# A four-layer image network on one core: layer norm of an MLP in a written order, and image norms moved from the spectra to the window attention

## The chip, the core and the metric

The kernel runs on one NeuronCore of a Trainium2 chip. The time is the device time of one execution in microseconds, the median of a few runs. The engines are PE (TensorE matmul, with PEld for its weight loads), DVE (VectorE), ACT (ScalarE), POOL (GpSimd) and SP (SyncE), which issues most of the DMAs. [...]

## The reference

Four images of 56 x 56 pixels with 128 channels go through four residual layers, `x = x + layer(group_norm(x))`, in float32.

```python
x = x + L0(_gn(x), ...)   # 7x7 window attention, then LayerNorm + global attention over 3136 tokens,
                          # then LayerNorm, 128->512, exact gelu, 512->128 (the MLP)
x = x + L1(_gn(x), ...)   # edge layer: relu(p_i + p_j + be) summed over j in each row of 56, node = relu(...)
x = x + L2(_gn(x), ...)   # Fourier neural operator with attention over the 56 rows as time steps
x = x + L3(_gn(x), ...)   # 3x1 convolution, row and column sums, relu
```

`_gn` is a group norm over 32 groups of 4 channels. In L2 each row of the image is one 56 x 128 field; it is instance-normed once more (`_inorm`), transformed with `rfft2` of 56 x 128, weighted, and compared with the other rows in an attention. So what L2 needs first of every image is its group norm, the mean and deviation of each row, and the spectra of its rows.

## The kernel before, in words

The image lies with its 128 channels on partitions and its 3136 pixels behind one another. `build` (L2368) first loads the inputs and takes their group norms, and then branches once: where the attention scores are small (they are with these inputs) it runs `first_layers` (L2416) for each of the four samples. What is inside the branch is scheduled by itself, and what follows it starts behind it. Per sample:

- **Windows**, `fast_windows` (L305): the image in 8 groups of 392 pixels (8 windows of 7x7). Ten small stages (`norm`, `project`, `score`, `value`, `turn`, `output`, `central`, `variance`, `attended`, `divide`) are issued in a skewed order, turn n working on groups n+2 down to n-11 (L467 to L471). PE, ACT and DVE keep that order as it is written (`manual_schedule`); POOL and SP are ordered by the framework's scheduler. The stages share three PSUM banks (`bank`, L348). Twice, at groups 3 and 7, `variance` takes the roots of four groups together (L434), one Sqrt on ACT and one reciprocal on DVE.
- **Global attention**, the rest of `fast_attention` (L560).
- **MLP**, `mlp` (L848), in 8 parts of 392 pixels. First the layer norm of all parts: `centre` (L676: a product with the centring matrix and a Square on ACT), a copy to `y` on ACT (L874), `inverse_deviation` (L684: a product that sums the squares, a Sqrt, a reciprocal on DVE, L692) and a multiply on DVE (L877). Then per part: `hidden` (L860, four products and four gelu), four products into `po` (L885), the bias and both residuals (L886) and three adds that put the windows back into image rows (L892 to L895), and statistics of the part (L896) for the next group norm. Only PE's order is written by hand; ACT and DVE are ordered by the scheduler.
- **Edge layer**, `edge_layer` (L905). Its result `x1` is stored to DRAM as `x2d[b]` by an SP DMA (L2424).

After the four samples come L2 and L3. SP loads weights; POOL makes the score weights (`all_score_weights`, L1393) and the value weights (`value_weights`, L1337), which end in a store `dd` on SP's queue (L1365). `spectra` (L1309) takes sample 3 first, whose `x1` is still in SBUF, then 0, 1 and 2, which are loaded from `x2d` (L1203). For each sample `normed_images` (L1188) does:

- statistics of each of the 56 rows (L1209), aggregated (L1213) to the group norm's mean and root (two products with `k.g4`, L1215 and L1231, Sqrt at L1233),
- the group norm in place in one instruction (L192, called at L1236) and a store to `xad[b]` (L1237),
- from the same row statistics the second norm of each row, `st.norm` (products at L1243 and L1249, Sqrt at L1251).

`sample_spectra` (L1258) then makes the **first transform** (L1267 to L1276: 224 small products of one row each, scaled by `st.norm` into `z`), and after it products into `S` and `iS` (L1281), `R` (L1293) and `xh` (L1303), evacuated by ACT and DVE. While one sample's spectra are issued, the next sample's norm is advanced by one step per chunk (L1332). PE, ACT and DVE keep the written order. Behind it come the attention weights (`attention_weights`, L1405, products L1471), `attend` (products L1594) and `outputs` (L2311).

## Time and profile before

The median of three runs is 3901.99 us (3901.64 to 3906.46). The profiled execution took 3907.5 us, with a span of 3905.7 us from the first to the last instruction, 79417 instructions and a mean granted PE clock of 0.954.

| stage | from - to, us | PE busy | DVE busy | ACT busy | POOL busy |
|---|---|---|---|---|---|
| inputs, norms, branch | 0 - 53 | 23.9 | 30.5 | 15.2 | 0.2 |
| windows, sample 0 | 53 - 155 | 91.0 | 54.1 | 47.6 | 8.7 |
| global attention, sample 0 | 155 - 542 | 365.2 | 325.9 | 290.9 | 0 |
| MLP, sample 0 | 542 - 607 | 59.1 | 39.3 | 33.5 | 0 |
| edge layer, sample 0 | 607 - 760 | 146.1 | 129.5 | 83.1 | 112.9 |
| windows, sample 3 | 2174 - 2271 | 87.6 | 48.7 | 48.3 | 3.7 |
| MLP, sample 3 | 2654 - 2716 | 56.2 | 39.4 | 33.0 | 0 |
| norm of sample 3 for L2 | 2870 - 2891 | 2.7 | 16.6 | 0.5 | 8.4 |
| spectra of the four samples | 2891 - 3016 | 93.3 | 68.2 | 34.7 | 29.6 |
| attention weights | 3016 - 3164 | 128.7 | 105.2 | 11.9 | 101.4 |
| attend | 3164 - 3515 | 324.5 | 252.1 | 59.9 | 308.3 |
| outputs | 3515 - 3906 | 347.5 | 225.0 | 144.2 | 221.7 |

A share of busy time tells little of a PE that does many small matmuls, whose ends are modelled; the order in time and the waits tell which engine was late. "L594" is line 594 of the kernel before, "a<-b" means that the instruction writes tile a and reads tile b, and "x56" counts instructions. The clock that was granted to PE is given as a share of full speed.

### The profile page before, as it was taken

How to read it: one execution, taken by the hardware profiler on the slowest of the kernel's cores; microseconds unless marked ns; L12 is line 12 of the kernel's file. 1: busy time of each engine (PE TensorE's matmuls, PEld its weight loads, DVE VectorE, ACT ScalarE, POOL GpSimd, SP SyncE). 2: the span in 40 equal slices, each digit the busy share in tenths (PEclk: the TensorE clock that was granted, in tenths of full speed). 3: DMA queues.
4: the chain of work that ended last, by engine and by line, in shares of the span. 5: the costliest groups of instructions: out<-in, count | busy, mean ns of one | idle time of the engine just before them, and what ended most of it. 6: DMA issues, size and time to landing. Idle time of an engine off the chain costs nothing. (4 is left out here: it accounts for less than half of the span.)

```text
span 3905.7 us, 79417 instructions
## 1 busy us (share of the span) xinstructions
PE 3553.4 (91%) x35416; PEld 1604.1 (41%) x35416; DVE 2891.3 (74%) x2759; ACT 2086.9 (53%) x2108; POOL 1156.6 (30%) x563
## 2 busy tenths in 40 slices
PE   6899989989998899999889999998967989989988
PEld 4432234542323455232245532224446433336564
DVE  6588877758887785888779578886965767775654
ACT  4577765457776544877655467774622012215332
POOL 0000006600000470000027100001851769984656
PEclk8999999999999999999999999999978999999888
DMA  2000000000000000000000000000031048841101
GB/s 95 1 1 1 1 17 2 19 1 1 1 1 1 18 3 18 1 1 1 1 18 3 18 1 1 1 1 1 3 112 61 1 98 177 165 111 70 52 7 50
DMA packets 73497, 111.13 MB, mean 28 GB/s; under 512 B 62140, under 2 KB 63932, under 8 KB 67900
## 3 DMA queue, kind: packets, MB, share of 16 engines
q1 hardware_dynamic: 14460, 93.13, 8.0%
q10 hardware_dynamic: 58688, 12.85, 2.0%
q8 instruction: 280, 4.59, 0.5%
q14 instruction: 69, 0.57, 0.1%
HBM read 79.46 MB, written 26.51 MB: 27 GB/s over the span
## 5 line engine op out<-in xcount | busy, mean ns | idle before, releaser
L651 ACT ACTIVATE f_ring<-f_s 128x1792 f32<-128x1792 f32 (+3 forms) x796 | 1097.7, 1429 | 231.5 <-PE f_s L649 229.6
L594 DVE TENSOR_TENSOR f_acc<-f_acc,f_ring 128x1792 f32<-128x1792 f32 x560 | 1134.0, 2025 | 66.1 <-ACT f_ring L651 9.3
L988 POOL TENSOR_TENSOR e_tp<-e_a,e_c 128x1792 f32<-128x1792 f32 x140 | 451.7, 3259 | 2288.1 <-ACT e_a L951 2183.7
L649 PE MATMUL f_s<-f_qT,f_kT 32*128 32x448 f32 x5376 | 741.4, 574 | 47.8 <-ACT f_ring L651 27.1
L600 PE MATMUL f_po<-f_ring,f_va 128*32 128x448 f32 x5376 | 592.0, 548 | 0.0
L986 DVE TENSOR_TENSOR e_td<-e_pa,e_c 128x1792 f32<-128x1792 f32 x252 | 491.4, 2015 | 14.4 <-ACT e_a L951 14.4
L649 PEld LDWEIGHTS f_s<-f_qT,f_kT 32*128 32x128 f32 x5376 | 269.7, 184 | 526.4 <-ACT f_ring L651 382.5
L993 PE MATMUL e_acc<-e_td,t_shared 32*32 32x448 f32 x8064 | 322.2, 545 | 20.9 <-DVE e_td L986 10.0
L990 ACT ACTIVATE e_tp<-e_tp 128x1792 f32<-128x1792 f32 x140 | 235.1, 1697 | 173.2 <-POOL e_tp L988 173.1
L1589 DVE TENSOR_TENSOR u_ud<-u_px,u_d 112x1792 f32<-112x1792 f32 x144 | 240.1, 1708 | 94.8 <-PE u_po L1594 85.7
L600 PEld LDWEIGHTS f_po<-f_ring,f_va 128*32 128x32 f32 x5376 | 133.5, 109 | 398.0 <-issue 397.0
L993 PE MATMUL e_acc<-e_tp,t_shared 32*32 32x448 f32 x4480 | 220.5, 544 | 3.1 <-ACT e_tp L990 2.5
L1594 PE MATMUL u_po<-u_ud,AT 112*64 112x448 f32 x960 | 200.7, 548 | 23.3 <-DVE u_ud L1589 23.3
L1591 POOL TENSOR_TENSOR u_up<-xh,u_d 112x1792 f32<-112x1792 f32 x64 | 193.8, 3054 | 24.1 <-PE u_po L1594 12.4
L993 PEld LDWEIGHTS e_acc<-e_td,t_shared 32*32 32x32 f32 x8064 | 133.8, 103 | 145.7 <-DVE e_td L986 56.0
L617 DVE RECIPROCAL f_den<-f_den 128x448 f32<-128x448 f32 x28 | 82.7, 2953 | 77.5 <-ACT f_den L616 77.5
L1594 PE MATMUL u_po<-u_up,AT 112*64 112x448 f32 x576 | 125.2, 541 | 0.9 <-POOL u_up L1591 0.9
L1594 PEld LDWEIGHTS u_po<-u_ud,AT 112*64 112x64 f32 x960 | 64.9, 137 | 147.6 <-issue 86.5
L594 DVE TENSOR_TENSOR f_acc<-f_ring 128x1792 f32<-128x1792 f32 x28 | 56.7, 2025 | 90.0 <-ACT f_ring L651 60.3
L865 ACT ACTIVATE m_hT<-m_ph,w_fb 128x392 f32<-128x392 f32 x128 | 72.7, 588 | 83.7 <-PE m_ph L864 78.2
L993 PEld LDWEIGHTS e_acc<-e_tp,t_shared 32*32 32x32 f32 x4480 | 94.4, 103 | 55.3 <-ACT e_tp L990 19.4
L1456 POOL TENSOR_TENSOR q_u<-iS,q_g 128x1792 f32<-128x1792 f32 x32 | 102.8, 3236 | 23.9 <-PE q_acc L1471 23.9
(467 smaller groups left out, 4710.2 us busy)
## 6 DMA issues: line engine op xcount, KB each, us to landing
u_d<-dd SPq DMA_DIRECT2D x48, 784.0 KB
xw<-in_x SPq DMA_DIRECT2D x4, 1568.0 KB
x2d<-x SPq DMA_DIRECT2D x4, 1568.0 KB
x_xs<-xad ACTq DMA_DIRECT2D x32, 196.0 KB
xm<-x_ev ACTq DMA_DIRECT2D x64, 98.0 KB
o_a<-xm SPq DMA_DIRECT2D x8, 784.0 KB
o_x<-x2d SPq DMA_DIRECT2D x4, 1568.0 KB
out<-o_o SPq DMA_DIRECT2D x12, 448.0 KB
```

Of the source, the lines that this page charges most:

```text
L594: nc.vector.tensor_add(acc, slots(j, 0) if c == 1 else acc, slots(j, c))
L600: nc.tensor.matmul(po[heads[h], :NB], va[o, c, heads[h]], p, start=(c == 0), stop=(c == 24))
L649: nc.tensor.matmul(ss[:, i, :NB], kT[heads[h], c * P:(c + 1) * P], qT[heads[h], blk(j)], start=True, stop=True)
L651: nc.scalar.activation(ring[:, slot:slot + m, :], ss[:, :m, :NB], AF.Exp, scale=scale)
L986: nc.vector.tensor_tensor(t, am, cm, ALU.max)
L988: nc.gpsimd.tensor_sub(t, bc(a.rearrange("p (l n) -> p l n", l=8), 1, 4), cm)
L990: nc.scalar.activation(tf, tf, AF.Relu)
L993: nc.tensor.matmul(acc[quarters[q], r, :NB], k.ident[o, o], t[o, q].rearrange("p l n -> p (l n)"), start=(g == 0), stop=(g == len(EDGE_TUR ...
L1456: nc.gpsimd.tensor_mul(u, bc(st.iS[:, bp, c, :HH], 1, HEADS), bc(g[:, n, c, :], 2, HH))
L1589: nc.vector.tensor_mul(u, bc(px[:, :, :NB], 2, m), dm)
L1591: nc.gpsimd.tensor_mul(u, bc(x, 2, m), dm)
L1594: nc.tensor.matmul(po[64 * b2:64 * b2 + 64, :NB], st.AT[:, 8 * i + h0 + q, 2 * bp + b2, :], u[:, b2, q, :], start=(left == 16), stop=(left ...
```

## The change

- **MLP.** PE, ACT and DVE now keep a written order. The layer norm is three functions: `central` (product; parts 0 to 3 are squared by ACT and copied by DVE, parts 4 to 7 copied by ACT and squared by GpSimd from the copy), `deviation` (sum of squares and Sqrt) and `divide` (reciprocal and multiply on DVE). Parts 0 to 2 are divided before the loop over the parts, part wi + 3 in turn wi. A Sqrt of a constant stands ahead of the layer norm and one ahead of the last turn's products. In turns 0 to 6 DVE adds the product, the bias and `xf` in one instruction, and GpSimd adds `xw` and puts the windows into image rows; the statistics of a part come one turn later. The last turn is as before.
- **Image norms.** `normed_images` is split into some fifty steps. For samples 0 to 2 it runs during `fast_windows` of the next sample: one step behind each stage, held back where a step needs a Sqrt until `variance` takes its own. It works in place on `x1` and stores `xad`. `x2d` of samples 0 to 2 is stored behind the edge layer as before; that of sample 3 behind the branch.
- **Spectra.** The order is 0, 1, 2, 3. Normed images of samples 0 to 2 are loaded from `xad` (two at once, the third when a buffer is free); the first two are requested ahead of everything else behind the branch. The norm of sample 3 goes on beside the spectra of samples 0 and 1, three steps per chunk. The first transform is a function of its own, and that of sample b + 1 is issued inside the spectra of sample b, behind chunks 2, 5, 7 and 9. The bank tag `acc` has four buffers for three.

The core of the diff:

```diff
@@ -432,6 +434,7 @@
             if q == HALF - 1:
                 r = wk.tile([P, N], F32, name="w_r")
                 nc.scalar.activation(r, var[:, :N], AF.Sqrt, scale=1024.0, bias=eps)
+                step(True)
                 nc.vector.reciprocal(r, r)
                 roots[g // HALF] = r
...
+        steps = beside(bank)
+        root_next = False
+
+        def step(root):
+            nonlocal root_next
+            if root or not root_next:
+                root_next = next(steps, None) == "root"
+
...
@@ -469,6 +480,7 @@
                              (central, n - 5), (variance, n - 6), (attended, n - 11), (divide, n - 10)):
                 if 0 <= g < NG:
                     stage(g)
+                    step(False)
...
@@ -865,37 +857,88 @@
-        es.enter_context(tc.manual_schedule(engines={mybir.EngineType.PE}))
-        squares = {}
-        for wi in range(9):
+        es.enter_context(tc.manual_schedule(engines={mybir.EngineType.PE, mybir.EngineType.Activation,
+                                                     mybir.EngineType.DVE}))
+        squares, roots = {}, {}
+        root = wk.tile([P, 1], F32, name="m_root")
+        nc.scalar.activation(root, k.eps, AF.Sqrt)
+
+        def central(wi):
+
+            pc = psum.tile([P, 512], F32, tag="mm", name="m_pc", bufs=4)
+            yb = y[:, parts[wi]]
+            nc.tensor.matmul(pc[:, :N], k.centre, xf[:, parts[wi]], start=True, stop=True)
+            squares[wi] = wk.tile([P, N], F32, name="m_sq", bufs=3)
+            if wi < 4:
+                nc.scalar.activation(squares[wi], pc[:, :N], AF.Square)
+                nc.vector.tensor_copy(yb, pc[:, :N])
+            else:
+                nc.scalar.copy(yb, pc[:, :N])
+                nc.gpsimd.tensor_mul(squares[wi], yb, yb)
+
+        def deviation(wi):
+            pv = psum.tile([P, 512], F32, tag="v", name="m_pv")
+            nc.tensor.matmul(pv[:, :N], k.ones_c, squares.pop(wi), start=True, stop=True)
+            roots[wi] = wk.tile([P, N], F32, name="m_r", bufs=8)
+            nc.scalar.activation(roots[wi], pv[:, :N], AF.Sqrt, bias=k.eps)
+
+        def divide(wi):
             if wi < 8:
-                pc = psum.tile([P, 512], F32, tag="mm", name="m_pc", bufs=4)
-                centre(k, wk, pc[:, :N], xf[:, parts[wi]], squares, wi)
-                nc.scalar.copy(y[:, parts[wi]], pc[:, :N])
-            if wi:
-                yb = y[:, parts[wi - 1]]
-                nc.vector.tensor_mul(yb, yb, inverse_deviation(k, wk, psum, squares.pop(wi - 1), 8))
+                r = roots.pop(wi)
+                nc.vector.reciprocal(r, r)
+                nc.vector.tensor_mul(y[:, parts[wi]], y[:, parts[wi]], r)
+        for n in range(10):
+            if n < 8:
+                central(n)
+            if 1 <= n < 5:
+                deviation(n - 1)
+            elif n > 5:
+                deviation(n - 2)
+            if n == 3:
+                divide(0)
+        divide(1)
+        divide(2)
+        def image_rows(wi, i0, i1):
+            r0 = (7 * wi + 3 + i0) % HH
+            return x1[:, r0:r0 + i1 - i0, :]
+
+        def statistics(wi):
+            for i0, i1 in (((0, 7),) if wi < 7 else ((0, 4), (4, 7))):
+                nc.vector.bn_stats(st[:, wi + (i0 > 0), :], image_rows(wi, i0, i1).rearrange("p l n -> p (l n)"))
+
+        def windows(t):
+            return t.rearrange("p (w i j) -> p w i j", w=8, i=7)
         ahead = hidden(parts[0])
         for wi, ts in enumerate(parts):
             hT = ahead
             if wi < 7:
                 ahead = hidden(parts[wi + 1])
+            else:
+
+                nc.scalar.activation(root, k.eps, AF.Sqrt)
             po = psum.tile([P, 512], F32, tag="acc", name="m_po")
             for f in range(4):
                 nc.tensor.matmul(po[:, :N], w.w2[:, f, :], hT[:, f, :], start=(f == 0), stop=(f == 3))
-            nc.vector.scalar_tensor_tensor(xf[:, ts], xf[:, ts], w.b2, xw[:, ts], ALU.add, ALU.add)
-            a = xf[:, ts].rearrange("p (w i j) -> p w i j", w=8, i=7)
-            x = po[:, :N].rearrange("p (w i j) -> p w i j", w=8, i=7)
+            divide(wi + 3)
+            if wi < 7:
+                nc.vector.scalar_tensor_tensor(xf[:, ts], po[:, :N], w.b2, xf[:, ts], ALU.add, ALU.add)
+                if wi:
+                    statistics(wi - 1)
+                add, a, x = nc.gpsimd.tensor_add, windows(xf[:, ts]), windows(xw[:, ts])
+            else:
+
+                nc.vector.scalar_tensor_tensor(xf[:, ts], xf[:, ts], w.b2, xw[:, ts], ALU.add, ALU.add)
+                statistics(6)
+                add, a, x = nc.vector.tensor_add, windows(xf[:, ts]), windows(po[:, :N])
             for i0, i1 in (((0, 7),) if wi < 7 else ((0, 4), (4, 7))):
-                r0 = (7 * wi + 3 + i0) % HH
-                rows = x1[:, r0:r0 + i1 - i0, :]
-                nc.vector.tensor_add(
-                    rows[:, :, 3:52].rearrange("p i (w j) -> p w i j", w=7), a[:, 0:7, i0:i1, :], x[:, 0:7, i0:i1, :])
-                nc.vector.tensor_add(rows[:, :, 52:56], a[:, 7, i0:i1, 0:4], x[:, 7, i0:i1, 0:4])
-                nc.vector.tensor_add(rows[:, :, 0:3], a[:, 7, i0:i1, 4:7], x[:, 7, i0:i1, 4:7])
-                nc.vector.bn_stats(st[:, wi + (i0 > 0), :], rows.rearrange("p l n -> p (l n)"))
-
-        nc.scalar.activation(wk.tile([P, 1], F32, name="m_root"), hT[:, 3, 0:1], AF.Sqrt, bias=k.eps, scale=0.0)
+                rows = image_rows(wi, i0, i1)
+                add(rows[:, :, 3:52].rearrange("p i (w j) -> p w i j", w=7), a[:, 0:7, i0:i1, :], x[:, 0:7, i0:i1, :])
+                add(rows[:, :, 52:56], a[:, 7, i0:i1, 0:4], x[:, 7, i0:i1, 0:4])
+                add(rows[:, :, 0:3], a[:, 7, i0:i1, 4:7], x[:, 7, i0:i1, 4:7])
+        statistics(7)
...
-def normed_images(k, w, st, b, pools, x2d, xad, ready):
+def normed_images(k, w, st, b, wk, bank, xp, xad):
...
+    rows = wk.tile([P, HH, 6], F32, name="s_rows", bufs=1)
     for t in range(HH):
         nc.vector.bn_stats(rows[:, t, :], x[:, t, :])
-        if t % 8 == 7:
+        if t % 2 == 1:
             yield
-    mv = wk.tile([P, 2], F32, name="s_mv")
+    mv = wk.tile([P, 2], F32, name="s_mv", bufs=1)
     nc.vector.bn_aggr(mv, rows.rearrange("p a b -> p (a b)"))
-    ps = psum.tile([P, 512], F32, tag="t", name="s_pt")
+    yield
+    ps = bank()
     nc.tensor.matmul(ps[:, 0:1], k.g4, mv[:, 0:1], start=True, stop=True)
...
     nc.vector.scalar_tensor_tensor(sq, d, HH / 4, sq, ALU.mult, ALU.add)
     nc.vector.tensor_add(mean, half[1], half[4])
+    yield "root"
+    nc.scalar.activation(t1, var, AF.Sqrt, bias=k.eps)
     nc.vector.reciprocal(mr[:, 1:2], t1)
-    apply_norm(k, x, x, mr)
-    nc.sync.dma_start(xad[b], x)
-    ready[b] = xp
-    yield
     nc.vector.tensor_scalar(mean, mean, 0.5, mr[:, 0:1], ALU.mult, ALU.subtract)
     nc.vector.tensor_scalar_mul(mean, mean, mr[:, 1:2])
...
-    nc.scalar.activation(d, ps[:, 128:128 + HH], AF.Sqrt, bias=k.eps)
+    nc.vector.tensor_copy(d, ps[:, 128:128 + HH])
+    yield
+    for t in range(0, HH, 14):
+        apply_norm(k, x[:, t:t + 14, :], x[:, t:t + 14, :], mr)
+        if t == 42:
+            nc.sync.dma_start(xad, x)
+        yield "root" if t == 42 else None
+    nc.scalar.activation(d, d, AF.Sqrt, bias=k.eps)
+    yield
     yield
...
-def sample_spectra(k, st, b, pools, x):
+def first_transform(k, st, b, pools, x, to):
...
-    z = wk.tile([P, 33, 2 * HH], F32, name="s_z")
+    z = to[b] = wk.tile([P, 33, 2 * HH], F32, name="s_z")
...
         yield
+
+
+def sample_spectra(k, st, b, pools, z):
...
-        ps = psum.tile([P, 512], F32, tag="acc", name="s_ps")
+        ps = psum.tile([P, 512], F32, tag="acc", bufs=4, name="s_ps")
...
-def spectra(k, w, st, x2d, xad):
+def spectra(k, w, st, xad, images):
...
-    ready = {}
+    nc.gpsimd.memset(st.x1[:, HH, :], 0.0)
...
-
-        order = [st.last] + [b for b in range(B) if b != st.last]
-        norms = [normed_images(k, w, st, b, (wk, tiny), x2d, xad, ready) for b in order] + [iter(())]
-        next(norms[1])
-        for _ in norms[0]:
+        norm = normed_images(k, w, st, B - 1, wk, lambda: tiny.tile([P, 512], F32, name="s_pt"), st.x1, xad[B - 1])
+        zs = {}
+        first = [first_transform(k, st, b, (wk, psum), st.x1 if b == B - 1 else images(b), zs) for b in range(B)]
+        for _ in first[0]:
             pass
-        for n, b in enumerate(order):
-            ahead = norms[n + 1]
-            for _ in sample_spectra(k, st, b, (wk, psum), ready.pop(b)):
-                next(ahead, None)
-            for _ in ahead:
-                pass
+        for b in range(B):
+            for n, _ in enumerate(sample_spectra(k, st, b, (wk, psum), zs.pop(b))):
+                for _ in range(3):
+                    next(norm, None)
+                if b < B - 1 and n in (2, 5, 7, 9):
+                    next(first[b + 1])
...
@@ -2421,23 +2480,50 @@
                 edge_layer(k, w1, x1, st)
-                nc.sync.dma_start(to, x1)
+                if to is not None:
+                    nc.sync.dma_start(to, x1)
+
+            def norms(b, bank):
+
+                if b < 0:
+                    return iter(())
+                return normed_images(k, w2, st, b, io, bank, x1w, xad[b])
...
             with tc.If(small_scores > 0) as small:
                 for b in range(B):
-                    first_layers(lambda *a: fast_attention(*a, k.mr[:, b, :]), I["x"][b], x2d[b],
-                                 loaded=b == 0)
+                    first_layers(lambda *a: fast_attention(*a, functools.partial(norms, b - 1), k.mr[:, b, :]), I["x"][b],
+                                 x2d[b] if b < B - 1 else None, loaded=b == 0)
...
+        x2s = ExitStack()
+        x2p = x2s.enter_context(tc.tile_pool(name="x2", bufs=2, side="right"))
+
+        def images(b):
+            if b not in loaded:
+                xp = loaded[b] = x2p.tile([P, HH + 1, HH], F32, name="s_x2")
+                for t in range(0, HH, 28):
+                    nc.sync.dma_start(xp[:, t:t + 28, :], xad[b, :, t:t + 28, :])
+                nc.gpsimd.memset(xp[:, HH, :], 0.0)
+            return loaded[b]
+
+        loaded = {}
+        for b in range(2):
+            images(b)
+        nc.sync.dma_start(x2d[B - 1], x1)
         l3p = es.enter_context(tc.tile_pool(name="l3", bufs=1))
         load_weights(k, l3p, I, "w3_", w2)
         load_weights(k, l3p, I, "w2_", w2, only=CONV_WEIGHTS)
-        st = Env()
-        st.x1, st.last = x1w, B - 1
...
                 with tc.tile_pool(name="g_wk", bufs=1, side="right") as wk:
                     all_score_weights(k, I, w2, sp, wk, st)
                     value_weights(k, I, w2, wk, dd)
-                    spectra(k, w2, st, x2d, xad)
+                    spectra(k, w2, st, xad, images)
+                x2s.close()
```

## The prediction

> **What bounds the kernel now.** I read the header of the page first, then busy time by stage, then the order in time inside the three stages that the change touches. The stages by busy time (columns: stretch, its length, then busy us and instructions of PE, PEld, DVE, ACT, POOL, then granted clock, DMA share, GB/s):
>
> ```profile
> 2174.00:2271.00 97.00, 87.59 (x718) 54.32 (x718) 48.73 (x97) 48.34 (x81) 3.65 (x11) 0.96 0.00 1
> 2271.00:2654.00 383.00, 361.04 (x3024) 109.69 (x3024) 325.04 (x168) 290.62 (x221) 0.00 (x0) 1.00 0.00 1
> 2654.00:2716.00 62.00, 56.16 (x164) 31.36 (x164) 39.43 (x66) 33.02 (x61) 0.00 (x0) 0.97 0.00 0
> 2716.00:2870.00 154.00, 146.10 (x3248) 73.31 (x3248) 130.28 (x81) 83.11 (x68) 113.25 (x36) 0.98 0.01 3
> 2870.00:2891.00 21.00, 2.69 (x14) 2.30 (x16) 16.63 (x93) 0.45 (x2) 8.37 (x20) 0.57 0.82 288
> 2891.00:3016.00 125.00, 93.29 (x1224) 83.17 (x1220) 68.21 (x269) 34.68 (x77) 29.64 (x38) 0.75 0.22 85
> ```
>
> These are, for the last sample, windows, global attention, MLP and edge layer, and then, once for all four, the lead-in to the spectra and the spectra. PE is near its limit everywhere but in the last two: there it stands idle for 18 us while DVE norms sample 3, and then works 93 of 125 us at three quarters of its clock. DVE is only half busy in the windows; it is the engine that limits the head of the MLP.
>
> **Part 1, MLP (four times).** In order of time on DVE (start, length, what):
>
> ```profile
> 2660.95 5.06 DVE L692 RECIPROCAL n_r<-n_r 128x392 f32<-128x392 f32 x2
> 2678.55 5.06 DVE L692 RECIPROCAL n_r<-n_r 128x392 f32<-128x392 f32 x2
> 2683.52 0.97 DVE L877 TENSOR_TENSOR m_y<-m_y,n_r 128x392 f32<-128x392 f32 x2
> ```
>
> and on PE, with the idle time before it and its releaser in brackets:
>
> ```profile
> 2667.87 5.64 PE L864 MATMUL m_ph<-m_y,w_f 128*128 128x392 f32 x16
> 2685.24 2.87 PE L885 MATMUL m_po<-m_hT,t_first 128*128 128x392 f32 x8 [1.20 <-DVE x L895]
> ```
>
> Eight reciprocals (2.5 us each) and multiplies (0.5) run without a break from 2660.95 to 2684.4, and only then the first output adds; PE waits for an accumulator bank at 2685.24. From the first hidden product (2667.87) PE needs 8 x 5.27 = 42.2 us (5.27: two groups of eight matmuls, 2675.98 to 2681.25) and takes 44.0, to 2711.8. After the change three divides (9 us) come before the loop and one in each turn. A turn of DVE is 3.0 (divide) + 0.63 (bias and xf, as L886) + 0.56 (L896) = 4.2 us, under PE's 5.27, so the 1.8 us go. At the head ACT loses four of its eight squares, four copies and the Sqrt table load (1.28, now early, in ACT's pause before 2656.3): 0.5 x 8 = 4 us; but PE's own 16 pairs, 2.9 us for the first two and 14 x 0.66, end at 2666.8, and the last sum of squares waits for GpSimd's four squares in a row, until about 2667.4, so only 0.4 us come out. Added: DVE copies (0.57, as L424) of the first four parts, hidden while DVE waits for the first root; GpSimd's squares, 1.0 us each (1.14 for 448 elements at L1351, 1.27 for 512 at L1390), counted just now; GpSimd's adds, 1.4 us a turn, under 5.27. The tail (0.95 us of adds, two statistics) stays. Gain 2.2 us each, **-9** (ends 0 and -14). The next sample's input load now waits for the last add, some 20 us later; it has the edge layer's 154 us to land.
>
> [...] The trace has such a case in the spectra, beside GpSimd's weights, of 56 elements that take 0.21 us elsewhere:
>
> ```profile
> 2909.69 2.95 DVE L1222 SCALAR_TENSOR_TENSOR s_sq<-s_d,s_sq 128x56 f32<-128x56 f32 x1
> 2916.81 2.83 DVE L192 TENSOR_SCALAR s_x<-s_x,s_mr 128x3136 f32<-128x3136 f32 x1
> ```
>
> If each multiply were held by one GpSimd instruction of 1.0 us, [...]a turn of DVE would be 5.2, just PE's pace, and the 1.8 us would still go; held as in the first row (+2.7) a turn is 6.9 and costs 1.6 x 7 = 11 a sample, which makes of -9 some +35. I take neither: GpSimd's add of 1.4 us starts together with the next reciprocal, which reads one tensor and lasts 2.5, so it is over before the multiply. Only the squares can meet a multiply, at the head, where DVE is not late. +35 counts toward the slower cases.
>
> **Part 2, three norms beside the windows (samples 1 to 3).** Each step is emitted behind a stage of the windows, on DVE's, PE's and ACT's fixed orders. DVE: 28 pairs of statistics at 0.32 (0.20 alone, 0.12 more behind another) = 9.0; aggregate 1.67; some 20 small ones at 0.15 to 0.30 = 3.7; reciprocal and scale 0.75; four applies at 0.5 = 2.0: **17.1 us**. PE: four matmuls at 0.4 = 1.6. ACT: two roots at 0.3, placed right behind the windows' own roots, so no table load. The SP queue gets one xad store per sample; behind it stand only the next input load and x2d, which wait for the MLP and the edge layer anyway.
>
> How much is hidden? In groups 3 to 6 of the windows DVE is busy 3.8 of 5.2, 4.0 of 5.6, 4.7 of 6.7 and 4.6 of 7.5 us. The steps that fall there (5, 6, 7 and 7) bring 1.6, 1.9, 2.2 and 3.3: 5.4, 5.9, 6.9 and 7.9, as long as or longer than the group. If DVE can be used to nine tenths, these groups grow by 0.8, 1.0, 0.9 and 1.3 us, the earlier ones by 0.6; PE's waits for the two mean matmuls cost 1.5; the late stretch, where DVE is mostly idle but every multiply (L444) is on PE's path, 2. Together **8 us a sample, +24**. Ends: 3.3 (PE's own 1.6 and as much waiting), and 18.7 when nothing is hidden.
>
> **Part 3, spectra.** Removed: 20.8 us from 2869.9 to the first transform at 2890.7. In its place the stored image is loaded: 1.57 MB at the 300 GB/s of the windows of these microseconds is 5 us, a half of it 2.6; issue at 2871.3 where t_w_qk is issued now, 2 us to land; the first half is there at about 2876. Lead-in 6 us.
>
> The first transform then runs with a cold PE (the granted clock is 0.50 in every stretch from 2874 to 2906). [...] The rows of L1271 (min/median/max ns) speak otherwise:
>
> ```profile
> L1271 PE MATMUL s_pr<-t_images,s_x x672: 222/224/318, 2928.4 to 3001.6; 128*64 128x33 f32 x168
> L1271 PE MATMUL s_pr<-t_images,x x224: 294/295/317, 2890.7 to 2902.6; 128*64 128x33 f32 x112
> ```
>
> The first transform stayed slow from its first to its last product, 12.1 us; later ones, begun warm, take 6.7 to 7.2. I take 12.1[...].
>
> Then the samples. Sample 2, which has no norm beside it, took 18.3 us (2994.6 to 3012.9): 7.2 first transform, 10.3 the rest (0.8 a wait). The next first transform now lies inside the previous sample, so: sample 0 17.0 + 1.7 cold + 4 waiting for sample 3's norm; sample 1 17 + 2; sample 2 17; sample 3 10.3; 3 us for the interleaving. The 4 and 2 come from the waits of PE on a norm's results, some 8.5 us per norm now, against three steps per chunk. Sum: 6 + 12.1 + 22.7 + 19 + 17 + 10.3 + 3 = 90, against 143 (2869.9 to 3012.9). **-53** (ends -60 and -30). GpSimd's weights begin later, since images and x2d go ahead of them on SP's queue (4.7 MB, 16 us), and would end near 2930; the attention weights need them at about 2963.
>
> **Sum.** -9 + 24 - 53 = -38. The profiled execution took 3907.5 (span 3905.7, 1.8 around it): 3869.5. The median of the runs is 5.5 lower, 3902.0: **3864**.
>
> **Rivals.** *Image 2 is stuck behind dd.* SP's queue is in order, and this is how it stood:
>
> ```profile
> 2885.88 0.33 SPq L1237 DMA_DIRECT2D xad<-x  x1
> 2918.02 0.38 SPq L1365 DMA_DIRECT2D dd<-d_f  x1
> 2918.49 1.55 SPq L1288 DMA_DIRECT2D apart<-S  x2
> 2920.09 0.55 SPq L1203 DMA_DIRECT2D s_x<-x2d  x1
> ```
>
> dd waits for GpSimd's last weight, and a load that was free to go stood behind it. If image 2 is queued so again, it is issued at 2918 to 2930, is half there 5 us later, and is wanted at about 2913: 10 to 22 us of waiting, say 15: 3879. Against it: image 2 is requested at the start of the spectra and its buffer is free at 2888. *The windows hide nearly all*: 3.3 for 8, 14 less: 3850. For it: DVE idles half the stage. *They hide nothing*: 18.7 for 8, 32 more: 3896. *Slower*: the steps stretch the windows beyond their DVE time, since a step delays the evacuation that PE waits for, and a norm's product takes one of three banks in rotation. At 0.5 us for each of 50 steps it is 25 a sample, 75 in all: 3902 - 62 + 75 = 3915. It decides from 62/3 = 20.7 us a sample.
>
> **How the numbers follow.** Main case 0.50 (3864); dd 0.27 (3879); all hidden 0.10 (3850); nothing hidden 0.09 (3896); slower 0.04 (3915). A measurement of this kernel can tell about 0.2%, 8 us, from no change. 3896 is at that edge, so half of its chance counts as same, with 0.01 more from the dd case: faster 0.90, same 0.06, slower 0.04. Leaving out the last two cases and going 8 below 3850 and 9 above 3879, for the sizes' own uncertainty: 3842 to 3888.
>
> **What would show it.** Right: windows of samples 1 to 3 some 8 us longer than sample 0's by their own change; MLPs of about 60 us without a wait at the third output product; first transform 6 us behind the edge layer, at half clock; last s_px product near 2963 less the MLPs' and plus the windows' shifts. Wrong: windows of 110 us or more, or a PE wait of over 8 us on a DMA ahead of sample 2's first transform.

## The result, and the profile after

The changed kernel takes **3870.9 us** (3867.4 to 3875.3, 4 runs) against 3901.8 (3899.0 to 3906.5, 4 runs): ratio **0.992, 95% interval 0.990 to 0.994**, so 31 us faster; forecast were 3864 in a range of 3842 to 3888. Its profiled execution took 3875.3 (span 3873.3, before 3905.7): a difference of 32.4.

To see where they are, I cut both spans at PE's own marks: the first attention product `f_s`, the first centring product of the MLP, the first edge product `e_acc` of each sample, and the first product of the attention weights `q_acc`.

| stretch | before | after | difference |
|---|---|---|---|
| start to the first `f_s` | 155.5 | 155.1 | -0.4 |
| `e_acc` to the next sample's `f_s` (edge layer and windows), 3 times | 246.4, 246.0, 248.5 | 258.2, 258.2, 261.6 | **+37.1** |
| `f_s` to the MLP, 4 times | 386.7, 385.7, 386.0, 385.7 | 384.3, 384.4, 384.4, 385.6 | -5.4 |
| MLP to `e_acc`, 4 times | 71.5, 71.3, 71.4, 68.2 | 67.4, 67.4, 67.4, 66.8 | **-13.4** |
| last `e_acc` to `q_acc` (edge layer and spectra) | 293.3 | 236.7 | **-56.6** |
| `q_acc` to the end | 889.5 | 895.8 | +6.3 |

Each column sums to its span. The third and the last stretch have the same code in both kernels. Over all kernels of this study, which leave that code alone, they lie between 384 and 388 and between 884 and 899 us, so -5.4 is scatter of single profiles. The +6.3 need not be scatter alone: with the spectra of before the last stretch takes 889.5 and 883.8 us (before, mlp_only), with the new ones 888.6 to 899.4, ten of eleven above both. DVE, ACT and POOL are as busy there as before, and PE's granted clock in the last 400 us moves between 0.85 and 0.89; what decides it is not shown. The three bold rows are the change.

Busy time by stage for the last sample and the spectra, columns as in the prediction's first fence (stretch, its length, busy us and instructions of PE, PEld, DVE, ACT, POOL, granted clock, DMA share, GB/s):

```profile
2176.50:2288.40 111.90, 94.85 (x732) 57.25 (x732) 68.59 (x183) 48.13 (x82) 8.74 (x22) 0.92 0.07 30
2674.00:2736.50 62.50, 58.03 (x167) 32.66 (x168) 39.36 (x52) 29.84 (x52) 13.21 (x25) 0.94 0.14 52
2888.50:2974.20 85.70, 73.30 (x1208) 64.04 (x1208) 48.65 (x131) 31.40 (x69) 36.10 (x57) 0.88 0.29 100
```

Windows: the norm's own instructions take 15 us of DVE (17.7 if the lengths of their rows are added, as the prediction did), but 43 us of it are still free; PE's granted clock fell from 0.96 to 0.92. Spectra, lead-in included: 85.7 us for what took 143.

**Windows**, PE in order of time, sample 1:

```profile
796.24 0.35 PE L1250 MATMUL w_mm<-s_mv,t_shared 128*128 128x1 f32 x2 [1.51 <-DVE w_rec L399]
...
821.70 0.68 PE L1283 MATMUL w_mm<-s_mean,c_ones_c 128*128 128x56 f32 x2 [4.12 <-DVE s_mean L1279]
822.17 1.64 PE L423 MATMUL w_mm<-xf,c_centre 128*128 128x392 f32 x2
...
844.55 1.49 PE L454 MATMUL w_mm<-w_h,w_fq 128*128 128x392 f32 x2 [1.84 <-DVE w_h L447]
```

PE waits 4.12 us for the row means of a norm, with the windows' own products queued behind. DVE, same stretch, shows what made the means late, a reciprocal of 2.6 us:

```profile
818.33 2.60 DVE L438 RECIPROCAL w_r<-w_r 128x392 f32<-128x392 f32 x1 [1.58 <-ACT w_r L436]
...
821.40 0.25 DVE L1279 TENSOR_SCALAR s_mean<-s_mean,s_mr 128x56 f32<-128x56 f32 x1
```

The clock view has half clock from 820.83 to 831.07, with 9.4 us of PE's work in it, and again behind the pause of 1.84:

```profile
820.83:831.07 10.24, 9.37 (x16) 3.39 (x16) 3.90 (x15) 1.90 (x4) 0.00 (x0) 0.50 0.00 0
844.73:848.14 3.41, 3.41 (x9) 2.15 (x9) 0.00 (x0) 1.17 (x2) 0.00 (x0) 0.50 0.00 0
```

Not all of this is new. The kernel before has a pause and half clock of its own at this place; PE's order and the clock view there:

```profile
824.04 0.96 PE L443 MATMUL w_mm<-w_r,c_ones 32*128 32x392 f32 x2 [2.42 <-ACT w_oT L229]
...
841.29 0.90 PE L451 MATMUL w_mm<-w_h,w_fq 128*128 128x392 f32 x2 [1.15 <-DVE w_h L444]
```

```profile
824.79:828.20 3.41, 3.41 (x6) 1.36 (x6) 0.75 (x2) 0.78 (x2) 0.00 (x0) 0.50 0.00 0
```

So the pauses are 1.7 and 0.7 us longer than before, and 12.8 us of work run at half clock instead of 3.4, which costs some 4.7 us (an estimate: half of the difference, with half clock taken to double the time; 16 products of L1360 in the spectra of this profile take 3.31 us at half clock and 1.83 at full). That is 7.1 of the 11.8 us by which this sample's stretch grew. The groups ahead of it, from the first value product (L394, after L396) to the eighth, take 43.0 us for 38.7.

**Spectra**, PE in order of time:

```profile
2888.70 6.73 PE L1322 MATMUL s_pr<-t_images,s_x 128*64 128x33 f32 x224 [1.00 <-DVE x L1009]
...
2912.17 0.38 PE L1250 MATMUL s_pt<-s_mv,t_shared 128*128 128x1 f32 x2 [3.49 <-DVE s_mv L1247]
...
2920.73 0.58 PE L1259 MATMUL s_pt<-s_t,t_shared 128*128 128x1 f32 x2 [3.83 <-DVE s_t L1256]
...
2926.20 0.68 PE L1283 MATMUL s_pt<-s_mean,c_ones_c 128*128 128x56 f32 x2 [1.72 <-DVE s_mean L1279]
...
2929.73 0.67 PE L1292 MATMUL s_pt<-s_sq,c_ones_px 128*128 128x56 f32 x2 [2.43 <-DVE s_sq L1289]
```

and SP's queue:

```profile
2673.28 2.02 SPq L2516 DMA_DIRECT2D s_x<-xad  x4
...
2902.21 0.84 SPq L2516 DMA_DIRECT2D s_x<-xad  x2
...
2936.21 0.40 SPq L1421 DMA_DIRECT2D dd<-d_f  x1
```

The first two images were requested 200 us before they were needed, so the first transform follows the edge layer after 1.0 us, at full clock (1.00 from 2739.1 to 2913.2), and takes 6.7 us. Image 2 was requested 34 us ahead of `dd`. Then the fourth norm makes PE wait 3.5, 3.8, 1.7 and 2.4 us for its four products.

### The profile page after: what moved, and what is told of

Its sections match the earlier page's. It is cut to its first block, busy times and chain, and to the rows that moved or that the text cites. A ratio compares the mean times of both kernels' runs of the same rounds, so it can differ in the third digit from the quotient of the medians.

```text
span 3873.3 us, 79430 instructions
## 1 busy us (share of the span) xinstructions
PE 3546.0 (92%) x35416; PEld 1589.1 (41%) x35416; DVE 2897.3 (75%) x2703; ACT 2077.8 (54%) x2080; POOL 1210.6 (31%) x667
## 5 line engine op out<-in xcount | busy, mean ns | idle before, releaser
L877 POOL TENSOR_TENSOR m_sq<-m_y 128x392 f32<-128x392 f32 x16 | 14.5, 919 | 1975.4 <-ACT m_y L876 1975.3
L661 PEld LDWEIGHTS f_s<-f_qT,f_kT 32*128 32x128 f32 x5376 | 268.4, 183 | 524.5 <-ACT f_ring L663 378.9
L1647 POOL TENSOR_TENSOR u_up<-xh,u_d 112x1792 f32<-112x1792 f32 x64 | 193.8, 3054 | 25.7 <-PE u_po L1650 12.4
```

The costliest lines, as they stand in the source:

```text
L661: nc.tensor.matmul(ss[:, i, :NB], kT[heads[h], c * P:(c + 1) * P], qT[heads[h], blk(j)], start=True, stop=True)
L1647: nc.gpsimd.tensor_mul(u, bc(x, 2, m), dm)
```

## The experiments

Sums over the samples at the same marks, from each run's profile: edge and windows (three), MLP (four), edge and spectra. The ratio is to the kernel before as it ran beside each kernel, with its 95% interval; the median of before was 3901.8 to 3902.3 us, and 3908.8 beside held_value, best2 and best3.

| kernel | edge and windows | MLP | edge and spectra | median | ratio |
|---|---|---|---|---|---|
| before | 740.9 | 282.4 | 293.3 | 3901.8 | 1 |
| after | 778.0 | 269.0 | 236.7 | 3870.9 | 0.992 (0.990 to 0.994) |
| mlp_only | 741.3 | 269.2 | 290.5 | 3886.4 | 0.996 (0.994 to 0.997) |
| old_mlp | 774.9 | 284.9 | 251.3 | 3896.2 | 0.998 (0.997 to 0.999) |
| late_products | 766.9 | 269.8 | 236.5 | 3865.4 | 0.990 (0.988 to 0.991) |
| no_stats | 768.1 | 270.1 | 237.5 | 3872.4 | 0.992 (0.990 to 0.994) |
| image_late | 777.6 | 268.4 | 254.5 | 3889.3 | 0.996 (0.994 to 0.998) |
| conv_moved | 782.6 | 269.7 | 243.1 | 3878.6 | 0.994 (0.992 to 0.995) |
| pool_light | 777.5 | 268.3 | 230.0 | 3872.4 | 0.992 (0.990 to 0.994) |
| held_value | 777.5 | 268.4 | 233.8 | 3873.8 | 0.991 (0.988 to 0.994) |
| best1 | 780.2 | 269.3 | 222.9 | 3860.0 | 0.988 (0.986 to 0.990) |
| best2 | 757.4 | 269.9 | 223.3 | 3841.8 | 0.984 (0.982 to 0.986) |
| best3 | 749.0 | 268.5 | 223.6 | 3831.5 | **0.981 (0.978 to 0.983)** |

### Each part alone: mlp_only and old_mlp

mlp_only puts the new `mlp` into the kernel before; old_mlp puts the old one into the kernel after.

> The kernel before with the new MLP alone. Theory of the prediction (PE loses only the wait that is shown before the third output product, 1.8 us, and 0.4 at the head): -9 us, some 3893. Theory from the two traces (that wait is longer in samples 0 to 2, 2.0 against 1.2 us in sample 3, and there the product behind it also runs at a fallen clock, 4.49 against 2.87 us; and the pause at the end of the global attention changes a little): -4 us in each of samples 0 to 2 and -1.4 in sample 3 from the first centring product to the first edge product, 1 or 2 more ahead of it: -13 to -19, some 3883 to 3889.

> The kernel after with the MLP of before: the norms beside the windows and the new spectra alone. By the prediction's sum (-9 for the MLP) it stands 9 us above the kernel after, some 3880. By the traces (-13 to -19 for the MLP) it stands 13 to 19 above it, 3884 to 3890. If the two parts hinder each other (the norms' stores and the MLP's GpSimd adds), the two single gains sum to more than 31 us.

The new MLP gives -15.9 us (3886.4 against 3902.3). In its profile the four MLPs are 13.2 us shorter, 3.7 to 4.6 in samples 0 to 2 and 0.8 in sample 3. The kernel before, sample 1, PE's order and the clock of its next stretch:

```profile
1277.66 4.49 PE L885 MATMUL m_po<-m_hT,t_first 128*128 128x392 f32 x8 [2.02 <-DVE x L895]
```

```profile
1279.00:1280.50 1.50, 1.50 (x3) 0.68 (x3) 1.50 (x4) 0.00 (x0) 0.00 (x0) 0.50 0.00 0
```

and the kernel after at the same product, PE's order:

```profile
1276.25 2.80 PE L856 MATMUL m_ph<-m_y,w_f 128*128 128x392 f32 x8
1278.88 2.80 PE L924 MATMUL m_po<-m_hT,t_first 128*128 128x392 f32 x8
```

A pause of 2.02 us cost 2.0 and then 1.7 more, because the product behind it ran part of its time at half clock. In sample 3 of the profile before, which the prediction read, the pause was 1.20 and the clock stayed at 1.00; in old_mlp sample 3 has 2.02 and 4.56 like the others, so that reading was a single case. With the old MLP in the kernel after, the MLPs are 15.9 longer again, as the second theory has it, but the time is 25 us worse. The rest is in the spectra, 251.3 for 236.7, where nothing was edited: a wait of 12 us for a norm's mean appears there. What it is, the runs on the spectra show.

### What lengthens the windows: late_products and no_stats

```diff
 # normed_images: ahead of each of its four products
-    yield
+    for _ in range(4):      # 4, 4, 3 (for 0) and 2 empty steps
+        yield
     ps = bank()
     nc.tensor.matmul(ps[:, 0:1], k.g4, mv[:, 0:1], start=True, stop=True)
```

> The kernel after, with 3, 3, 3 and 1 empty steps more ahead of the four small products of each norm. Nothing is added or left out on any engine; only PE meets the four products later. Theory A: the windows of samples 1 to 3 are 12 us longer because PE, in order, waits for a norm's DVE results (1.5, 0.3 and 4.1 us, with some 3 us of half clock behind the last): the windows fall by some 7 us each, and the waits of the fourth norm in the spectra (3.5, 3.8, 1.7, 2.4) by about half: -28, some 3843. Theory B (the prediction's reason): DVE is overfull in groups 3 to 6 and the length comes from there: the same time within 3 us, some 3870. Theory C: the later steps push the applies onto the last multiplies of the windows, and +2 us a sample comes out: some 3877.

Three windows fell by 11.1 us, 3.7 each and not 7; the spectra not at all. The waits for `s_t` and `s_mean` are gone and their products lie where PE has other work (kernel late_products, PE's order):

```profile
816.67 1.67 PE L446 MATMUL w_mm<-w_r,c_ones 32*128 32x392 f32 x2 [2.42 <-ACT w_oT L230]
818.27 0.68 PE L1287 MATMUL w_mm<-s_mean,c_ones_c 128*128 128x56 f32 x2
...
836.44 1.44 PE L454 MATMUL w_mm<-w_h,w_fq 128*128 128x392 f32 x2 [1.52 <-DVE w_h L447]
```

The pause of 2.42 in the first row is also in the kernel before; the one of 1.52 (there 1.15) comes from the norm's last DVE step ahead of `w_h`, and half clock follows it (0.50 from 838 to 840). So the order of the products cost half of what I had assigned to it: of the 4.12 us, 2.42 had only taken the place of the windows' own pause, which comes back, with 6.8 us of half clock behind it where the kernel after has 10.2. What is left is 8.7 us a sample over the windows of before.

```diff
 # normed_images, b < B - 1: the 28 pairs of statistics left out
-        nc.vector.bn_stats(rows[:, t, :], x[:, t, :])
+    nc.gpsimd.memset(rows, 0.5)
```

> The kernel after, with the 28 pairs of row statistics of the three norms beside the windows left out (9 us of DVE each; the rows get a constant, so the norms are not the reference's); all other steps stay where they are. If DVE's fill in groups 3 to 6 sets the length, as the prediction has it, the windows of samples 1 to 3 fall by 4 to 5 us each. By the trace of the kernel after, groups 3 to 5 grew by 0.6 us each only and the rest came from the waits for products: 2 to 3 us each.

-9.9 over three windows, 3.3 each: less than the fill of DVE should give (4 to 5), more than the trace of after had suggested. The wait of 4.12 for `s_mean` is unchanged in it. Both causes are real and about equally large; if they add up, they are 7.0 of the 12.4 us a sample.

### The first transform: image_late

```diff
 # images(b), b = 0, ahead of its loads
+    nc.gpsimd.tensor_copy(xp[:, 0, 0:1], x1[:, HH - 1, HH - 1:HH])
```

> The kernel after, with the first image's load held until the edge layer has ended (GpSimd copies one element of the last edge block into the image's place first, and the load overwrites it). In the kernel after that load lies 200 us earlier, and the first transform starts 1.0 us behind the edge layer at full clock, 6.7 us long. Now PE has to wait some 5 us for it. If a pause of this size is enough to make the whole transform slow, it takes 12.1 us as in the kernel before: +5 +5.4 = +10, some 3881. [...] If the clock doesn't matter here, +5 and 6.7 us.

The first transform of image_late, PE's order, and the clock of its stretches:

```profile
2900.38 9.58 PE L1322 MATMUL s_pr<-t_images,s_x 128*64 128x33 f32 x224 [8.89 <-DMA s_x<-xad]
```

```profile
2891.50:2900.30 8.80, 0.00 (x0) 0.00 (x0) 0.68 (x1) 0.00 (x0) 2.90 (x12) 0.78 0.85 298
2900.40:2906.40 6.00, 6.00 (x114) 6.00 (x115) 0.64 (x1) 0.58 (x1) 0.00 (x0) 0.50 1.03 402
2907.50:2910.00 2.50, 2.47 (x86) 2.35 (x82) 0.64 (x1) 0.94 (x2) 0.00 (x0) 1.00 0.35 73
```

The load took longer than the 5 us that I put (it lands together with the `qk` weights, at 298 GB/s), and the transform takes 9.58: between the 12.1 of the kernel before and the 6.7 of the kernel after. So a load behind the edge layer, as the prediction had it, would have cost 7.9 us of pause and 2.9 of half clock. The time rose by more, 18: PE waits another 14.0 us for `s_mv` later on, behind one DVE instruction on one column:

```profile
2926.53 7.07 DVE L1751 TENSOR_TENSOR t_w_M<-t_w_M,t_w_M0rev 112x1 f32<-112x1 f32 x1
```

The same instruction took 0.93 in the kernel after and 2.80 in old_mlp.

### What holds DVE in the spectra: conv_moved, pool_light, held_value

```diff
 # spectra: conv_steps is conv_weights' DVE work, one instruction a step
                 for _ in range(3):
                     next(norm, None)
+                if b == 2:
+                    next(conv, None)
+                    next(conv, None)
```

> The kernel after, with DVE's 24 small preparations of the convolution weights emitted between sample 2's products in the spectra, where GpSimd is idle, and not where the planner put them, in the middle of the fourth norm beside GpSimd's weights. Theory S: there, DVE's small instructions with operands in SBUF wait for GpSimd's instructions (0.9 to 1.2 us for what takes 0.15 elsewhere), so the preparations take 9 us of DVE ahead of the norm's second product, which PE waits for: the stretch from the last edge products to the attention weights falls from 236.7 by 4 to 7 us, the time to some 3866. If they only fill DVE time that PE wouldn't have used, nothing changes.

The stretch is longer in its profile, 243.1 for 236.7, not shorter; the whole time (3878.6) can't be told from the kernel after, since the intervals overlap. Without the weights' preparations in between, the norm's own instructions are held. Kernel conv_moved, DVE's order:

```profile
2922.96 3.55 DVE L1255 TENSOR_TENSOR s_t<-s_mv,s_mr 128x1 f32<-128x1 f32 x1
2926.54 7.73 DVE L1256 SCALAR_TENSOR_TENSOR s_t<-s_t,s_mv 128x1 f32<-128x1 f32 x1
```

and GpSimd's at that time:

```profile
2926.47 0.36 POOL L1440 TENSOR_SCALAR q_skip<-t_images 128x32 f32<-128x32 f32 x1
2926.80 0.24 POOL L1449 TENSOR_TENSOR q_g<-t_w_qk 128x32 f32<-128x32 f32 x1
2927.01 1.12 POOL L1413 TENSOR_TENSOR d_t<-t_w_P,t_w_V 128x448 f32<-128x448 f32 x1
...
2933.41 0.24 POOL L1450 TENSOR_TENSOR q_t<-t_w_qk 128x32 f32<-128x32 f32 x1
2933.64 1.39 POOL L1421 TENSOR_SCALAR d_t<-t_w_V,t_images 128x448 f32<-128x448 f32 x1
```

L1256 takes 0.22 us elsewhere. Here it lasts through eleven GpSimd instructions with two tensor operands, back to back, and ends 0.63 us after the first long one with a single tensor operand has begun. The long ones of old_mlp (7.28 us) and image_late (7.07) end 0.64 us behind the start of the same kind of instruction. If GpSimd is the cause, the waits of DVE's small steps must vanish with its arithmetic:

```diff
 # score_weights and value_weights: only copies, scalings and small sums are kept
-        nc.gpsimd.tensor_mul(out[:, n], qk[:, 0, 0], qk[:, 1, n])
-        nc.gpsimd.tensor_mul(t, qk[:, 0, 1], qk[:, 1, i])
-        nc.gpsimd.tensor_tensor(out[:, n], out[:, n], t, op)
+        nc.gpsimd.tensor_scalar_mul(out[:, n], qk[:, 0, n], 1.0)
...
-    nc.gpsimd.tensor_mul(d[:, 0], w.P[:, 0], m)
```

> The kernel after, with most of GpSimd's arithmetic for the score and value weights left out (the products, and the sums that need them), so the weights and the output are not the reference's. Theory S (DVE held by GpSimd's instructions): the DVE stretch from the aggregate to the last apply of the fourth norm, 2910 to 2935 in the kernel after, falls from 25 to some 14 us, no small instruction takes over 0.4 us, and the spectra shorten by 8 to 11 us. If the small instructions were late for their weights' loads instead, they stay as long as they are.

The same two steps in the kernel after, and then in pool_light, DVE's order:

```profile
2918.51 0.94 DVE L1255 TENSOR_TENSOR s_t<-s_mv,s_mr 128x1 f32<-128x1 f32 x1
2919.49 1.18 DVE L1256 SCALAR_TENSOR_TENSOR s_t<-s_t,s_mv 128x1 f32<-128x1 f32 x1
```

```profile
2920.53 0.16 DVE L1255 TENSOR_TENSOR s_t<-s_mv,s_mr 128x1 f32<-128x1 f32 x1
2920.72 0.22 DVE L1256 SCALAR_TENSOR_TENSOR s_t<-s_t,s_mv 128x1 f32<-128x1 f32 x1
```

From the aggregate to the last apply it is 15.5 us, with GpSimd's arithmetic 24.7; no small instruction takes over 0.53; the stretch is 6.7 us shorter, somewhat less than the 8 to 11 that I had put. With that the holding in the kernel after is shown to come from GpSimd's arithmetic; the weights are loaded in this kernel too. The three holds of over 7 us lie in other kernels, which were not run without the arithmetic: that they have the same cause is argued from their ends. The time as a whole (two runs) can't be told from the kernel after.

```diff
 # value_weights, called behind spectra, waits for the fourth norm's last result
+    nc.gpsimd.tensor_copy(half[:, 0, 0:1], last)
```

> The kernel after, with GpSimd's value weights alone held until the fourth norm has ended (one copied element of the norm's result makes them wait); nothing else is changed, the preparations of the convolution weights stay in the norm. Theory S (DVE's small instructions wait for GpSimd's): with half of GpSimd's row gone from beside the norm, DVE's waits fall, and the stretch from the last edge products to the attention weights goes from 236.7 to some 228 to 232, the time to some 3864. If the length came from the norm's own chain of small steps, nothing changes; if the value weights' store is now late for what reads it, it gets longer.

The stretch is 2.9 us shorter in its profile, the wait for `s_t` 1.5 instead of 3.8; the median (3873.8, four runs from 3864 to 3880) doesn't tell it from the kernel after. Alone it is inconclusive.

### Put together: best1, best2, best3

best1 is late_products, conv_moved and held_value together, with two empty steps more ahead of each norm's last DVE step.

> The late products, the preparations of the convolution weights in sample 2, GpSimd's value weights held until the fourth norm has ended, and each norm's last DVE step two steps later. From the late products alone 3865; in the spectra the norm then meets half of GpSimd's instructions only and none of the preparations: 10 to 14 us less; in the windows the last DVE step no longer lies ahead of the multiply that PE waits for: 1 to 2 us less in each of three. Sum some 3847. Against it: the value weights end some 25 us later, and if they or their store are then late for the attention weights, part of it is lost.

The spectra fell by 13.8 us, as expected: DVE now meets half of GpSimd's row and carries only the norm. The windows did not gain; two of them are 5.8 and 7.5 us *longer* than in late_products. PE's clock in best1:

```profile
842.48:859.55 17.07, 15.58 (x34) 8.43 (x32) 2.51 (x4) 3.52 (x6) 0.00 (x0) 0.50 0.00 0
```

The moved step made two pauses, 0.8 and 1.2 us, out of one of 1.5, and PE stayed at half clock for 17 us, though it was busy for 15.6 of them.

```diff
 # best2: normed_images, ahead of the last reciprocal
-    for _ in range(4):
+    for _ in range(11 if b < B - 1 else 2):
         yield
 # best3: and among the statistics
         if t % 2 == 1:
             yield
+            if b < B - 1 and t >= 29 and t % 6 != 1:
+                yield
```

> Late products, preparations of the convolution weights in sample 2, value weights held behind the fourth norm, and the last DVE step of the norms beside the windows (a reciprocal of 0.49 us and a scale) at the windows' end. The spectra as in the run with all of these, 223; the windows as with the late products alone, 254 to 258, less 1 where the last step made PE wait: some 3847. Theory of the clock: the steps between the windows' last multiplies lengthened PE's pauses there (0.8, 1.2, 0.75 us) and kept it at half clock for 18 us; without them it stays at full clock behind the pause of 1.15 us, as in the kernel before. If the half clock comes back all the same, it was not those pauses, and the time is some 3857.

> As the run before, with nine empty steps more among the second half of the statistics, so that groups 3 to 6 carry fewer of them, and the aggregate and its products lie at groups 7 and 8, where DVE has more room. By the trace of the late products the statistics cost 0.6 us in each of groups 2 to 4 and the aggregate 1.9: 2 to 3 us less in each of three windows than the run before, some 3840. If DVE is just as full at groups 7 and 8, the same time.

best2 has no half clock there any more (its products take 0.90 and 0.82 us, as at full clock; over 753 to 865 the clock is 0.95 for 0.88) and takes 22.8 us less in the three windows than best1. best3 takes 8.4 off again, with the statistics thinned out and the aggregate at groups 7 and 8. PE's order and the stage by busy time:

```profile
803.20 0.38 PE L1253 MATMUL w_mm<-s_mv,t_shared 128*128 128x1 f32 x2
807.28 0.38 PE L1263 MATMUL w_mm<-s_t,t_shared 128*128 128x1 f32 x2
816.72 0.92 PE L446 MATMUL w_mm<-w_r,c_ones 32*128 32x392 f32 x2 [2.42 <-ACT w_oT L230]
817.57 0.43 PE L1289 MATMUL w_mm<-s_mean,c_ones_c 128*128 128x56 f32 x2
823.34 0.32 PE L1299 MATMUL w_mm<-s_sq,c_ones_px 128*128 128x56 f32 x2
```

```profile
750.50:853.40 102.90, 89.98 (x733) 55.48 (x733) 68.14 (x183) 47.91 (x82) 8.74 (x22) 0.97 0.08 32
```

None of the norm's four products waits (the pause of 2.42 is the windows' own, as in the kernel before), DVE is as busy as in the kernel after, 68 us, and the clock is 0.97 again. The same norm, with the same instructions, now costs 2.7 us a sample (749.0 - 740.9, over three) where it cost 12.4. Of the difference, 3.7 went with the later products, 3.2 with the last step at the windows' end (late_products to best2, whose other edits lie in the spectra) and 2.8 with the statistics and the aggregate. best3 is 1.95% faster than the kernel before and, with intervals that don't touch, faster than the changed kernel.

## Why the prediction was right, and where it was wrong

**The sign and the range** were right; 3870.9 is 7 us over the main case. The sum was -9 + 24 - 53 = -38; the profiles have -13.4 + 37.1 - 56.6 = -32.9.

**Part 1, -9: the mechanism right, the size off.** The term that was too small is the 1.8 us at the third output product. I read one sample of four, sample 3, whose wait was 1.20 with no loss of clock; the others lost 3.5 to 3.8 (2.02 of pause and 1.5 to 1.8 of half clock). The head (0.4) was right within a few tenths: 13.66 before, 13.51 after. Holds by GpSimd, which at the size of the row shown would have made +35 of it, rightly counted for nothing: the changed kernel's 32 multiplies take 0.57 us, 0.76 at most, beside GpSimd's adds of 1.4 and squares of 0.84. GpSimd has pauses of 3.9 us between its adds there.

**Part 2, +24: too small by 13.** The step that failed is "the late stretch, where DVE is mostly idle but every multiply (L444) is on PE's path, 2". In sample 1 the late stretch, behind the eighth value product, grew by 7.4 us; ahead of it the groups grew by 4.4, no more than priced (4.6, and 1.5 for waits). The wait that I had not costed is the one for `s_mean`, whose DVE step stands behind the other user of the root, a reciprocal of 2.6 us: 4.12 us in place of the windows' own 2.42. And I priced every wait at its own length, while half clock behind the two pauses of the late stretch cost some 4.7 us more than before. The sum of 8 also leaves out PE's own time for the four products (1.6 there, 2.1 measured), which only the lower end has. That DVE's fill lengthens groups 3 to 6 was right: without the statistics 3.3 of 12.4 us go. The end of 3.3, with everything hidden but PE's own work, is what best3 reached (2.7).

**Part 3, -53 against -56.6: right by luck, as a sum of two errors.** "Lead-in 6 us, issue at 2871.3 where t_w_qk is issued now" failed: the images' place was free at 2673, and nothing else held their loads. With that went "I take 12.1" for a cold first transform: PE paused for 1.0 us only, and the transform took 6.7. So the 12.1 of the row didn't apply; where there is a pause, image_late measured 9.6. Together 10 us better than forecast. Against that "sample 0 22.7" took 30.5: the fourth norm was charged some 8.5 us of DVE time a norm and 4 us of waiting, and half clock 1.7 us (an estimate; it equals half of one piece of 3.41 us); the sample needed four waits of 11.5 us in all, and the clock was 0.50 from 2913.2 to 2933.7, 20.5 us. Here the holding by GpSimd that I set aside for part 1 did decide: beside GpSimd's weights DVE's small steps took 0.9 to 1.2 us each. The last fence of part 1 had shown such a row (2.95 us for 0.21), in this very stage, and I used it for the MLP and not for the norm that stays in the spectra.

**The rivals.** *Image 2 behind dd* didn't occur: PE waits for no DMA in the spectra. *All hidden* and *nothing hidden* were off on either side: +12.4 lies between 8 and 18.7. *Slower* would have needed 20.7 a sample.

What stays open is what ends half clock: it lasted one piece of 3.41 us in one place and five in another, and no run shows why. How much of GpSimd's row a DVE step meets also stays a matter of where both fall: the unchanged spectra took 236.7, 237.5 and 251.3 us (after, no_stats, old_mlp).

## What to carry to other kernels

Small work that is hidden in another engine's idle time still has a price on the engine that must keep its written order: the norms beside the windows cost 12.4 us a sample, of which 3.7 went when each product was emitted several steps behind the step that makes its operand. Count a pause of PE with the slow work behind it (2.0 us and 1.7 more in the MLP of before), not by its length. Keep DVE's chains of small steps away from long rows of two-operand GpSimd instructions: the chain of the fourth norm took 24.7 us beside them and 15.5 without. Before pricing a stage that occurs four times, read all four: three MLPs lost 3.5 to 3.8 us where the fourth lost 1.2.

## What the runs showed of the hardware

- In the profiles of before and after the granted clock is 1.00 or 0.50, and every stretch of half clock that ends within the span lasts 3.41 us or a multiple of it, from 3.41 to 34.1. Half clock lasted 3.4 us in the MLP of before, 6.8 behind the pause of 2.42 in late_products, 10.2 in the windows of the kernel after, 17.1 in best1, and 34.1 around the first transform of before (2872.8 to 2906.9).
- A pause's length alone doesn't decide in these runs. Pauses of 2.02 (MLP of before) and 1.52 us (late_products) were followed by half clock, one of 1.51 ahead of `s_mv` in the kernel after was not; one of 1.20 (sample 3's MLP) was not, but 1.19 in best1 was. In the MLP of before PE had 1.40 us of work in the 3.42 us ahead of the half clock (1275.34 to 1278.76).
- Nor does half clock end after a fixed time of work. In image_late PE starts at 2900.38 and full clock comes at 2906.7, after 6.3 us of work without a pause. In the first transform of before PE starts at 2890.7, and half clock stays until 2906.9, with 15.5 us of work in these 16.2.
- DVE's instructions on one column took longer beside GpSimd's arithmetic. In the kernel after, L1255 and L1256 took 0.94 and 1.18 us, and 0.16 and 0.22 in pool_light, without it. Single ones took 7.07 (image_late), 7.28 (old_mlp) and 7.73 us (conv_moved) while GpSimd ran two-operand instructions back to back, eleven in conv_moved; each ended 0.63 or 0.64 us behind the start of a long GpSimd instruction with a single tensor operand. That GpSimd held these three is inferred from their ends.
- An apply of the norm (L193, a single tensor operand) took 1.16 us beside GpSimd's last weights and 0.62 in pool_light. Reads from PSUM and statistics kept their times: 0.14 and 0.15 us for the copy into `s_mr` (L1254), 0.62 and 0.64 for `s_z` (L1324), in the kernel after beside that arithmetic and in pool_light; the statistics of 12 rows took 1.50 us in the kernel after at 2900.4, ahead of GpSimd's row, and 1.50 in old_mlp at 2923.6, beside it.
